# Four edits in a graph network kernel: later row loads, tests on tiles of their own, one test moved between passes, and degree columns one slot later

## The chip, the cores and the metric

The kernel runs on one core of a Trainium2 chip. The metric is the device time of one execution in microseconds (us), and the median of several is compared. A core has a matrix engine (PE), a vector engine (DVE), a scalar engine (ACT), a general engine (GpSimd, POOL in the profile) and SyncE (SP), which here only issues DMA transfers. Each engine works through its own queue in order and waits on semaphores for the others.

## The reference, cut to what matters

There are 16 graphs with 1024 nodes of 128 features, and a dense adjacency of zeros and ones. Two blocks follow each other, each with a residual and a layer norm:

```python
# block 0: four gated layers per graph
for i in range(4):
    hw = einsum('bnc,cd->bnd', h, weight[i])
    m = einsum('bjn,bjd->bnd', adj, hw)
    h = gru_cell(m, h, w_ih[i], w_hh[i], b_ih[i], b_hh[i])
# block 1: neighbours are thinned row by row, then three mean-aggregation layers
for n in range(N):                       # earlier rows change later rows
    row = carry[n]; num = sum(row)
    sf = (num + 1) // 2 if num > 10 else 1
    rm = row & (cumsum(row) % sf == 0) & (num > 1)
    carry[n] = row & ~rm; carry[:, n] &= ~rm
deg = clip(sum(adj_d, -1), 1)
out = (adj_d @ x / deg) @ Wr + x @ Wx + b
h1 = batchnorm(relu(out / norm(out)))    # h2 and h3 likewise from h1 and h2
y = concat(h1, h2, h3) @ Wl + bl
```

The thinning of block 1 needs only the adjacency, not the result of block 0.

## The kernel before, in words

The program takes fast paths that hold only if every adjacency entry is 0 or 1. So it tests the adjacency in tiles of 128 rows by 1024 columns: one DVE instruction per tile (a `scalar_tensor_tensor`, `look`, line 1982) writes a flag into a column of `bad`, and a general routine runs at the end if any flag is set. Eight tiles a graph are tested, spread over three stages. Their only product is that flag.

**Gated stage** (`Gated` and `FixPoint`, to about 1345 us). `Gated.run` goes over pairs of graphs (`b0`), four layers, and two streams `s`, one graph each. `layer` multiplies the state by the adjacency tiles `h_a` (L1093: the state is split into a rounded part h_hi and a rest h_lo, the h_lo products follow the h_hi products) and then runs the gates (L1105 on PE, L1115 to L1124 on ACT, L1118, L1120 and L1133 on DVE, h_zh and h_h L1128 to L1134 on POOL). Between these pieces it calls `aside(n)`. `aside` advances the second program, `FixPoint.steps`, by one yield and runs jobs of the other stream: loads of the next graph's `h_a` and `h_x` (L1011, L1022) on POOL's queue, h_lo of a new graph on POOL (`begin_rows`, L1058), the addition for a finished graph (L1071). `FixPoint` thins the neighbours in 32 blocks of 128 rows of four graphs. Of each block, `load` (L687) brings four row tiles `f_a` (cast to bf16) on POOL's queue into a pool of eight; `keep` and `count` (L731, L739) count along rows; `settle`, `rows` (L868, L870) and `last_u` finish the block one turn later. `rows` gives `f_nr`, which SP stores to DRAM (L871) and reads back transposed for later blocks (`read_back`, L715). One block takes two layers, one of each stream, and 20 yields. In `before`, `last_u` issues the four loads of the block after next as soon as the rows of the old block have been used. The test of the gated stage (`check`, L1013) reads an `h_a` tile that is there for the matmuls, one per two layers: 32 tests, two a graph.

**First pass** (`Sage.first`, `slot`, to about 1855 us). One graph takes 16 slots, and everything is emitted slot by slot in a hand-written order that all five engines keep. In each slot `unit` turns a part of the thinned matrix into `p_at` (L1489 on PE, L1494 on DVE, L1497 on ACT) for the *next* graph and `pack` makes bytes of it on POOL (L1504). For the graph of *now*, `agg` multiplies (slots 0, 1, 3, 4 and 9 to 14), `degree_columns` (slots 3 and 6) turns the row of degrees into columns with four small matmuls (L1559) and takes the reciprocal on DVE (L1561, L1562), `out_first` (slots 5 and 7) makes `p_oa` and `p_ob`, and `scale_rows` (L1394, L1395, slots 6 and 8), `squares` (L1402 on ACT) and `rows` (L1408 to L1413 on DVE) normalise. `turn_x` (slots 6 and 8) transposes the next graph's input (L1424) and ACT copies it out (L1541). `degree_columns`, `turn_x` and `turn_r` share one PSUM buffer, s_tr. Four adjacency tiles a graph are loaded on SP (`load_a`, L1465) into four buffers and tested (L1985).

**Second pass** (`Sage.second`, `slot_second`, to about 2140 us). Eight slots a graph: `out_next` (L1765 to L1771), `chain` (scale and squares), `rows`, `turn_r`, the products with `q_at` (L1808), and `unpack` (L1755 on ACT, L1757 on POOL and DVE), which turns bytes back into `q_at`. Two adjacency tiles a graph go through one buffer `q_a` (loads L1794, tests in slots 3 and 7).

A **third pass** and an output stage follow without tests.

Of the kernel before, what the change touches and what calls it, by code (L numbers as in the profile page):

```python
# [22 lines left out]
B = 16  # L23
# [607 lines left out]
class FixPoint:  # L631
# [110 lines left out]
    def steps(self):  # L742

        nc, G = self.nc, self.G
        for c in range(G):
            self.load(c)
        old = None
        for i, (k, b0) in enumerate(self.todo):
            diag = slice(k * P, k * P + P)

            yield
            if old:
                old.settle()
                old.wide_u(0)
            yield
            if old:
                old.wide_u(1)
                old.rows(0)
            yield
            if old:  # L760
                old.wide_u(2)
                old.rows(1)
            yield
            if old:
                old.rows(2)
                old.wide_u(3)
                old.rows(3)
            a = [self.loaded.pop((i, g)) for g in range(G)]
            pt = self.ps.tile([P, G, P], F32, name="f_pd")
            turned = pt.rearrange("p g n -> p (g n)").bitcast(BF)[:, :G * P].rearrange("p (g n) -> p g n", g=G)  # L770
            for g in range(G):
                nc.tensor.transpose(turned[:, g, :], a[g][:, diag], self.cst["ident_b"])
            yield
            if old:
                old.last_u()

            both = self.small.tile([P, G, P], BF, name="f_both")
            for g in range(G):
                nc.vector.tensor_mul(both[:, g, :], a[g][:, diag], turned[:, g, :])
            nc.gpsimd.affine_select(both, both, pattern=[[0, G], [1, P]], compare_op=ALU.is_gt, fill=0.0,  # L780
                                    base=0, channel_multiplier=-1)
            self.turn(i, 0)
            yield
            rank = self.two.tile([P, G, N], F16, name="f_rank")
            self.keep(i, a[0])
            self.count(i, 0, a[0], rank, pt)
            yield
            yield
            self.turn(i, 1)
            self.keep(i, a[1])  # L790
            yield
            self.count(i, 1, a[1], rank, pt)
            if i == 0:

                for c in range(G, self.LOTS):
                    self.load(c)
            yield
            yield
            yield
            self.turn(i, 2)  # L800
            self.keep(i, a[2])
            self.count(i, 2, a[2], rank, pt)
            yield
            for g in range(G):
                self.read_back(i + 1, g)
            yield
            self.turn(i, 3)
            self.keep(i, a[3])
            self.count(i, 3, a[3], rank, pt)

            num = self.sm[:, 0, 0, :]
            nc.vector.tensor_scalar(num, rank[:, :, N - 1], 1.0, None, op0=ALU.mult)
            q = self.params(num, 0)
            u = self.diag_u(rank[:, :, diag], q)
            if old:
                old.check()
            yield
            x = self.removed(u, q, both)
            yield
            yield  # L820
            pd, num = self.less(x, rank, 1)
            rd = self.small.tile([P, G, P], F16, name="f_rd")
            q = self.params(num, 1, lambda: nc.vector.tensor_sub(rd, rank[:, :, diag], pd))
            u = self.diag_u(rd, q)
            yield
            x = self.removed(u, q, both)
            yield
            old = self.Block(self, i, a, rank, both, x)
            yield
        yield  # L830
        old.settle()
        for n in range(4):
            old.wide_u(n)
            if n < 3:
                yield
            old.rows(n)
        yield
        old.last_u()
        yield
        old.check()  # L840

    class Block:
# [30 lines left out]

        def last_u(self):
            fix = self.fix
            for g in range(fix.G):
                fix.load(fix.G * self.i + g + fix.LOTS)
            self.u = fix.small.tile([P, fix.G, P], F16, name="f_u3", bufs=1)
            fix.diag_u(self.rank[:, :, self.diag], self.q, self.u)

# [43 lines left out]
class Gated:  # L924
# [45 lines left out]
    def prepare(self):  # L970
# [21 lines left out]
            nc.vector.tensor_copy(dst, pt[:, :L0 * 3])  # L992
        nc.vector.tensor_add(self.bs, self.bi, self.bh)

    def stream(self, s):
        return self.Stream(self, s)

    class Stream:
# [9 lines left out]
        def load_adj(self, b, j):  # L1008
            if b < B:
                self.adj[j] = self.top.adjp.tile([P, N], FR, name=f"h_a{self.s}")  # L1010
                self.nc.gpsimd.dma_start(self.adj[j], self.top.adj[b, j * P:(j + 1) * P, :].bitcast(FR))  # L1011

        def check(self, b, j):  # L1013
            junk = self.top.wk.tile([P, N], BF, name="h_junk", bufs=1)
            self.nc.vector.scalar_tensor_tensor(junk, self.adj[j].bitcast(F32), 0.0, self.adj[j].bitcast(F32),
                                                op0=ALU.is_gt, op1=ALU.not_equal,
                                                accum_out=self.top.bad[:, tile_of(b, j):tile_of(b, j) + 1])

        def load_x(self, b):
            if b < B:  # L1020
# [145 lines left out]
    def beside(self, st, ot, l, s, b0, steps):  # L1166


        before = l if s == 0 else l + 1
        if before in (0, L0):  # L1170
            old = not (s == 0 and b0 == 0)
            new = not (s == 1 and b0 + 2 >= B)
            jobs = {5: [], 7: [], 9: []}
            nxt = ot.b + 2 if old else ot.b

            def begin():
                ot.b = nxt
                ot.begin(0)

            if old:  # L1180
                jobs[5].append(lambda: ot.finish(0))
                jobs[7].append(lambda: ot.finish(1))
                jobs[0] = [lambda: ot.load_x(nxt)]
                for j in range(4, NB):
                    jobs.setdefault(j // 2 - 2, []).append(lambda j=j: ot.load_adj(nxt, j))
            if new:
                jobs.setdefault(5 if old else 0, []).append(lambda: ot.begin_rows(nxt))
                jobs[9].append(begin)
        else:
            jobs = {5: [lambda: ot.next_layer(0)], "rest": [lambda: ot.rest(0)],  # L1190
                    7: [lambda: ot.next_layer(1)], 8: [lambda: ot.rest(1)]}

        if l == L0 - 1:

            for j in range(4):
                jobs.setdefault(4, []).append(lambda j=j: st.load_adj(st.b + 2, j))

        checked = []

        def aside(n):  # L1200

            first = n == 7 and before not in (0, L0)
            if not first and n not in ("rest", 8):
                next(steps, None)
            for job in jobs.get(n, ()):
                job()
            if n == 1 and s == 1 and not checked:
                own = l in (0, L0 - 1)
                (st if own else ot).check((st if own else ot).b, l // 2)
                checked.append(l)  # L1210
            if first or n == 8:
                next(steps, None)
        return aside


class Sage:
# [388 lines left out]
    def slot(self, b, t):  # L1605
# [2 lines left out]
        now, nxt = b >= 0, n < B  # L1608

        if nxt:  # L1610
            if t in (0, 2, 8):
                self.load_a(n, (0, 2, 8).index(t) + 3)
            if t in (4, 6):
                self.load_nr(n + 1, (t - 4) // 2)
            if t == 7:
# [15 lines left out]
        if now:  # L1631
# [3 lines left out]
            if t in (0, 1, 3, 4):  # L1635
                f, lo = t // 3, t in (1, 4)
                if not lo:
                    g["pa", f] = bank()
                self.agg(g["pa", f], (self.xh, self.xl)[lo], g["at"], f, range(NB), not lo, lo)
            if t in (5, 7):  # L1640
                self.out_first(b, t // 7)
            if t in (6, 8):
                f = t // 8
                g["o", f] = self.scale_rows(b, f, g.pop(("oa", f)), g.pop(("ob", f)))
            if t in (3, 6):
                self.degree_columns(b, t // 6)
            if t in (7, 9):
                f = t // 9
                g["r", f] = self.rows(b, f, g.pop(("o", f)), g.pop(("ss", f)))
# [14 lines left out]
        if nxt:  # L1664
# [5 lines left out]
                self.turn_x(n, t // 8)  # L1670
            if t in (7, 12):
                self.split_x(n, t // 12)
            if t in (4, 10, 12, 14):
                self.check(n, (4, 10, 12, 14).index(t) + 2)

        if now:
            if t == 2:
# [104 lines left out]
    def slot_second(self, b, t):  # L1782
        nc, g, p = self.nc, self.g.get(b), self.g.get(b - 1)
        acc = lambda b, f: self.acc[:, b, 4 * f:4 * f + 4, :]
        if b < B:
# [2 lines left out]
                self.load_bytes(b + 1, 0)  # L1788
            if t == 3:
                self.load_bytes(b, 1)  # L1790
            if t in (0, 4):
                k = 6 + t // 4
                g["a", k] = self.wk.tile([P, N], F32, name="q_a", bufs=1)
                nc.sync.dma_start(g["a", k], self.adj[b, k * P:(k + 1) * P, :])  # L1794
            if t in (0, 3):
# [38 lines left out]
            self.unpack(b - 1, t + 5)  # L1834
        if t == 5 and b < B:
            self.split(1, g["r", 1], g["rh"], g["rl"])
        if t in (3, 7) and b < B:
            k = 6 + t // 7
            a = g.pop(("a", k))
            look(nc, a.bitcast(BF).rearrange("p (n h) -> p n h", h=2)[:, :, 0], self.bad, a, b, k)  # L1840
        if t == 7 and b < B:
# [229 lines left out]
```

## Time and profile before

| | us |
|---|---|
| median of 3 runs | 2366.65 |
| lowest and highest | 2364.03, 2367.73 |
| the profiled execution | 2359.65 |
| its span in the trace | 2357.6 |

| engine | busy us | share of the span |
|---|---|---|
| PE | 2173.6 | 92% |
| DVE | 1952.1 | 83% |
| ACT | 1327.9 | 56% |
| POOL | 1060.6 | 45% |

All durations come from one profiled execution. A line of a timeline gives the start in us from the span's start, the duration in us, the engine, the line of the program, the operation, what is written and read, and how many were merged; in brackets stands the idle time of the engine ahead of it and what ended it. A line of the list of waits gives engine, tile and line, what was waited for, and then the us in total, how many times, and the longest. A line of the windows by stage gives the stretch, its length, the busy us of PE, PE's weight loads, DVE, ACT and POOL with instruction counts, the granted PE clock, the DMA share and GB/s. The page's chain of the work that ended last holds only one instruction for this kernel (u_y on ACT), so that the stages have to be read one by one.

### The profile page before, as it was taken

What the parts mean: (1) busy time and instruction counts of PE and PEld (TensorE: products, weight loads), DVE (VectorE), ACT (ScalarE), POOL (GpSimd) and SP (SyncE); (2) the same over time, 40 slices, a digit from 0 to 9 for tenths busy, and PEclk for the clock granted to TensorE, in tenths of its full rate; (3) what the DMA queues carried; (4) which work ended last, traced back from release to release, by engine and by line L of the source; (5) the groups of instructions that cost most, each with busy time, mean ns of one, the idle gap of its engine ahead of it and who ended that gap; (6) DMA issues with size and microseconds to landing.
All of it is one profiled execution on the core that took longest, in us unless ns stands there. A gap on an engine that the chain in (4) does not pass through costs nothing. (4 is left out here: it accounts for less than half of the span.)

```text
span 2357.6 us, 33315 instructions
## 1 busy us (share of the span) xinstructions
PE 2173.6 (92%) x10665; PEld 1483.7 (63%) x10665; DVE 1952.1 (83%) x4338; ACT 1327.9 (56%) x3238; POOL 1060.6 (45%) x1092
## 2 busy tenths in 40 slices
PE   6999999999999999999999888888898888888987
PEld 4665655656656656556566467777777666666765
DVE  4998998989989989989989977777777587886777
ACT  3556565655556465565656556556655344445756
POOL 4436346354364363363553265555555245451002
PEclk9999999999999999999999989999999899999989
DMA  7337245263363364271552376666665587775414
GB/s 229 78 80 228 56 122 167 54 196 104 85 202 77 93 191 93 72 216 41 160 153 66 134 256 241 227 233 244 241 241 186 183 288 265 287 264 182 127 39 144
DMA packets 209790, 385.70 MB, mean 164 GB/s; under 512 B 59074, under 2 KB 80228, under 8 KB 209604
## 3 DMA queue, kind: packets, MB, share of 16 engines
q1 hardware_dynamic: 163780, 263.90, 33.1%
q0 software_dynamic: 41472, 117.46, 18.7%
q10 hardware_dynamic: 4352, 2.11, 0.4%
q8 instruction: 86, 1.41, 0.2%
q14 instruction: 100, 0.82, 0.1%
HBM read 307.71 MB, written 109.25 MB: 177 GB/s over the span
## 5 line engine op out<-in xcount | busy, mean ns | idle before, releaser
L1105 PE MATMUL h_g<-h_h,h_wh 128*128 128x512 f32 x768 | 399.3, 601 | 3.0 <-DVE h_r L1118 3.0
L1105 PE MATMUL h_g<-h_ms,h_wi 128*128 128x512 f32 x768 | 392.2, 592 | 0.0
L739 DVE TENSOR_TENSOR_SCAN f_rank<-f_a,f_first,f_pd 128x1024 f16<-128x1024 bf16 x128 | 299.2, 2343 | 3.2
L1093 PE MATMUL h_g<-h_a,h_lo 128*128 128x512 f32 x1024 | 275.3, 408 | 25.6 <-POOL h_lo L1058 25.6
L1134 POOL TENSOR_TENSOR h_h<-h_zh,h_r 128x512 f32<-128x512 f32 x126 | 205.0, 1627 | 194.8 <-DVE h_r L1133 175.7
L1093 PE MATMUL h_g<-h_a,h_hi 128*128 128x512 f32 x1024 | 284.1, 419 | 1.5 <-DMA h_a<-in_adj_dram 1.5
L1105 PEld LDWEIGHTS h_g<-h_ms,h_wi 128*128 128x128 f32 x768 | 145.6, 190 | 183.9 <-issue 166.6
L1504 POOL CAST p_b<-p_at 128x512 uint8<-128x512 f32 x256 | 187.2, 741 | 118.3 <-ACT p_at L1497 48.9
L1093 PEld LDWEIGHTS h_g<-h_a,h_lo 128*128 128x128 f32 x1024 | 195.7, 195 | 69.4 <-POOL h_lo L1058 28.6
L1402 ACT ACTIVATE s_junk<-s_o 128x128 bf16<-128x128 f32 x384 | 113.9, 298 | 213.5 <-DVE s_o L1395 202.6
L1093 PEld LDWEIGHTS h_g<-h_a,h_hi 128*128 128x128 f32 x1024 | 190.2, 190 | 62.3 <-issue 20.1
L1128 POOL TENSOR_TENSOR h_zh<-h_z,h_h 128x512 f32<-128x512 f32 x63 | 80.1, 1272 | 320.6 <-ACT h_z L1124 320.6
L1096 ACT COPY h_ms<-h_g 128x512 f32<-128x512 f32 x128 | 73.7, 576 | 224.8 <-PE h_g L1093 179.4
L1105 PEld LDWEIGHTS h_g<-h_h,h_wh 128*128 128x128 f32 x768 | 129.1, 190 | 85.8 <-issue 65.2
L1121 ACT ACTIVATE h_r<-h_r,h_bi 128x512 f32<-128x512 f32 x128 | 92.3, 721 | 131.2 <-DVE h_r L1120 131.0
L916 ACT ACTIVATE f_u<-f_rank,f_q 128x128 f16<-128x128 f16 (+7 forms) x128 | 110.5, 866 | 76.6 <-DVE f_rank L854 76.6
L1494 DVE SCALAR_TENSOR_TENSOR p_at<-p_nr,p_u 128x128 fp32r<-128x128 bf16 (+1 forms) x192 | 103.4, 546 | 46.9 <-PE p_u L1489 46.9
L1497 ACT ACTIVATE p_at<-p_u 128x512 fp32r<-128x512 f32 (+3 forms) x160 | 74.5, 470 | 119.9 <-DVE p_at L1494 77.9
L687 POOL DMA_DIRECT2D f_a<-in_adj_dram x128 | 69.6, 545 | 122.9 <-DVE f_nr L870 57.0
L1768 PE MATMUL q_ob<-s_wxp,q_xt 128*128 128x256 f32 x512 | 122.9, 383 | 0.0
L1489 PE MATMUL p_u<-ident_b,p_nr 128*128 128x128 bf16 x1024 | 103.4, 230 | 18.6 <-ACT p_at L1497 16.1
L893 ACT ACTIVATE f_pd<-f_rank,f_q 128x128 f32<-128x128 f16 x128 | 59.1, 462 | 106.7 <-DVE f_q L701 103.5
(260 smaller groups left out, 5049.3 us busy)
## 6 DMA issues: line engine op xcount, KB each, us to landing
h_a<-in_adj_dram POOLq DMA_DIRECT2D x128, 512.0 KB, 7.9
f_a<-in_adj_dram POOLq DMA_DIRECT2D x128, 256.0 KB, 7.3
e_nr<-f_nr SPq DMA_DIRECT2D x128, 256.0 KB
p_nr<-e_nr SPq DMA_DIRECT2D x32, 1024.0 KB
p_a<-in_adj_dram SPq DMA_DIRECT2D x64, 512.0 KB
s_at<-p_b SPq DMA_DIRECT2D x32, 512.0 KB
s_ag<-s_ag SPq DMA_DIRECT2D x64, 256.0 KB
q_agi<-s_ag SPq DMA_DIRECT2D x32, 512.0 KB
```

The source lines that it names most:

```text
L739: nc.vector.tensor_tensor_scan(out, a, other[:, 0, 0:1].to_broadcast([P, N]), start, op0=ALU.add, op1=ALU.bypass)
L916: nc.scalar.activation(u[:, :n1], rank[:, g, :n1], AF.Abs, bias=q[:, 1, g:g + 1], scale=q[:, 0, g:g + 1])
L1093: nc.tensor.matmul(pm[f], part[:, j, :], st.adj[j][:, half[f]], start=(j == 0 and n == 0), stop=(j == NB - 1 and n == 1))
L1105: nc.tensor.matmul(pg, lhs, rhs, start=(i == 0), stop=(i == len(mm) - 1))
L1121: nc.scalar.activation(r, r, AF.Tanh, bias=bias(self.bi, 2))
L1128: aid.tensor_tensor(zh, z, h, ALU.mult)
L1134: aid.tensor_tensor(h, zh, r, ALU.subtract)
L1402: self.nc.scalar.activation(junk, o[:, i, :], AF.Square, accum_out=ss[:, i:i + 1])
L1489: nc.tensor.matmul(pu[:, i * P:(i + 1) * P], v[:, 4 * f + i, j * P:(j + 1) * P], self.cst["ident_b"], start=True, stop=True)
L1494: nc.vector.scalar_tensor_tensor(at[:, j, c0:c0 + low], v[:, j, c0:c0 + low], 0.0, pu[:, :low], op0=ALU.is_lt, op1=ALU.is_lt)
L1504: self.nc.gpsimd.tensor_copy(g["b", f][:, j, :], g["at"][:, j, f * HF:(f + 1) * HF].bitcast(F32))
L1768: nc.tensor.matmul(pb[:, i], g["xt"][:, f, blk], self.wxp, start=(i % 2 == 0), stop=False)
```

## The change

It makes four edits. (1) In `FixPoint.steps` the four row loads are issued from the step that follows the second count of the block, instead of from `last_u` earlier in the same block: the same tiles, six yields later. (2) In the gated stage the 32 tests read tiles of their own: `load_test` loads a float32 tile on SP's queue into one buffer `h_test`, at `aside(3)` of stream 0's layer, and `check` tests it at `aside(1)` of stream 1's layer, where the old test stood. The `h_a` loads lose their `bitcast` of the source to float32r. (3) Of the second pass's two tests per graph the one in slot 3 goes, with its load, and the first pass gets one more: it now loads at slots 0, 3, 5, 8 and 12 and tests at slots 2, 4, 10, 12 and 14. (4) The second `degree_columns` of a graph moves from slot 6 to slot 7, ahead of `out_first`.

```diff
@@ FixPoint.steps
             yield
             yield
+            if old:
+                for g in range(G):
+                    self.load(G * (i - 1) + g + self.LOTS)
             yield
             self.turn(i, 2)
@@ Block.last_u
             fix = self.fix
-            for g in range(fix.G):
-                fix.load(fix.G * self.i + g + fix.LOTS)
@@ Gated
+    def load_test(self, n):
+        if n < B * 2:
+            self.test = self.wk.tile([P, N], F32, name="h_test", bufs=1)
+            self.nc.sync.dma_start(self.test, self.adj[n // 2, n % 2 * P:(n % 2 + 1) * P, :])
+
+    def check(self, n):
+        junk = self.wk.tile([P, N], BF, name="h_junk", bufs=1)
+        look(self.nc, junk, self.bad, self.test, n // 2, n % 2)
@@ Stream.load_adj
-                self.nc.gpsimd.dma_start(self.adj[j], self.top.adj[b, j * P:(j + 1) * P, :].bitcast(FR))
-
-        def check(self, b, j):
...
+                self.nc.gpsimd.dma_start(self.adj[j], self.top.adj[b, j * P:(j + 1) * P, :])
@@ Gated.beside, aside
+            if n == 3 and s == 0:
+                self.load_test(b0 // 2 * L0 + l)
             if n == 1 and s == 1 and not checked:
-                own = l in (0, L0 - 1)
-                (st if own else ot).check((st if own else ot).b, l // 2)
+                self.check(b0 // 2 * L0 + l)
                 checked.append(l)
@@ Sage.slot
-            if t in (0, 2, 8):
-                self.load_a(n, (0, 2, 8).index(t) + 3)
+            if t in (0, 3, 5, 8):
+                self.load_a(n, (0, 3, 5, 8).index(t) + 3)
...
+            if t == 7:
+                self.degree_columns(b, 1)
             if t in (5, 7):
                 self.out_first(b, t // 7)
...
-            if t in (3, 6):
-                self.degree_columns(b, t // 6)
+            if t == 3:
+                self.degree_columns(b, 0)
...
-            if t in (4, 10, 12, 14):
-                self.check(n, (4, 10, 12, 14).index(t) + 2)
+            if t in (2, 4, 10, 12, 14):
+                self.check(n, (2, 4, 10, 12, 14).index(t) + 2)
@@ Sage.slot_second
-            if t in (0, 4):
-                k = 6 + t // 4
+            if t == 0:
+                k = NB - 1
...
-        if t in (3, 7) and b < B:
-            k = 6 + t // 7
+        if t == 7 and b < B:
+            k = NB - 1
```

More of the change, by code (lines that the diff above doesn't have):

```diff
@@ L1010, in load_adj @@
                 self.adj[j] = self.top.adjp.tile([P, N], FR, name=f"h_a{self.s}")
-                self.nc.gpsimd.dma_start(self.adj[j], self.top.adj[b, j * P:(j + 1) * P, :].bitcast(FR))
-        def check(self, b, j):
[L1014 to L1017, printed above, removed]
+                self.nc.gpsimd.dma_start(self.adj[j], self.top.adj[b, j * P:(j + 1) * P, :])
         def load_x(self, b):
```

## The prediction

> **What bounds the kernel now.** First the windows by stage: share of time in which each engine is busy.
>
> ```profile
> 400.00:600.00 200.00, 195.93 (x773) 119.92 (x772) 181.11 (x378) 116.86 (x219) 92.83 (x92) 0.98 0.42 111
> 1500.00:1600.00 100.00, 90.08 (x628) 72.28 (x626) 71.34 (x184) 58.71 (x164) 55.28 (x65) 0.95 0.70 250
> 1900.00:2000.00 100.00, 87.14 (x465) 67.94 (x464) 80.20 (x130) 45.75 (x147) 49.12 (x35) 1.00 0.81 278
> ```
>
> PE is the busiest engine in the gated stage (98%), the first pass (90%) and the second (87%), so the end moves by what happens to PE's gaps. The list of waits, second, says what ends them:
>
> ```profile
> PE h_g L1093 <- POOL h_lo L1058: 25.6, 7, 3.7
> PE s_tr L1424 <- DVE s_rdeg L1561: 29.9, 15, 2.0
> PE q_ag L1808 <- DVE q_at L1757: 22.3, 14, 1.9
> ```
>
> Each has one place per graph or pair of graphs. The timelines there, third. Gated stage, POOL at one change of graphs:
>
> ```profile
> 351.41 0.53 POOL L687 DMA_DIRECT2D f_a<-in_adj_dram  x1 [2.16 <-DMA h_a<-in_adj_dram]
> ...
> 356.71 0.53 POOL L687 DMA_DIRECT2D f_a<-in_adj_dram  x1 [1.01 <-DMA h_a<-in_adj_dram]
> 357.24 0.65 POOL L780 TENSOR_SCALAR_AFFINE_SELECT f_both<-f_both 128x512 bf16<-128x512 bf16 x1
> 357.84 1.26 POOL L1071 TENSOR_TENSOR h_x<-h_x,h_w 128x512 f32<-128x512 f32 x1
> 359.07 2.49 POOL L1058 TENSOR_TENSOR h_lo<-h_x,h_hi 128x512 fp32r<-128x512 f32 x2
> ```
>
> Four row loads wait in turn for older loads to land; h_lo stands behind them, and PE (ready at 356.7) behind h_lo until 360.38. First pass, PE and ACT in slots 6 and 7 of one graph:
>
> ```profile
> 1598.99 0.25 PE L1559 MATMUL s_tr<-s_one,p_rl 1*128 1x1 f16 x4
> 1601.23 0.66 PE L1424 MATMUL s_tr<-ident,p_s 128*128 128x128 f32 x4 [1.99 <-DVE s_rdeg L1561]
> ...
> 1601.95 1.11 PE L1581 MATMUL p_oa<-s_wr,s_ag 128*128 128x128 f32 x8
> ```
> ```profile
> 1601.14 0.31 ACT L1402 ACTIVATE s_junk<-s_o 128x128 bf16<-128x128 f32 x1 [3.38 <-DVE s_o L1395]
> ...
> 1602.57 0.57 ACT L1541 COPY p_xt<-s_tr 128x512 f32<-128x512 f32 x1
> ```
>
> PE idles 1.99 us for the one s_tr buffer; ACT's copy of that buffer comes only after the squares (L1402). Second pass, DVE:
>
> ```profile
> 2008.88 1.39 DVE L1985 SCALAR_TENSOR_TENSOR q_a<-q_a 128x1024 bf16<-128x1024 f32 x1
> ...
> 2010.58 1.23 DVE L1410 TENSOR_TENSOR s_ss<-s_ss,mask 128x4 f32<-128x4 f32 x1
> 2011.91 1.40 DVE L1413 SCALAR_TENSOR_TENSOR s_r<-s_o,s_ss 128x512 f32<-128x512 f32 x1
> ...
> 2015.00 2.16 DVE L1985 SCALAR_TENSOR_TENSOR q_a<-q_a 128x1024 bf16<-128x1024 f32 x1 [0.24 <-DMA q_a<-in_adj_dram]
> ```
>
> Here PE idles 1.57 + 0.48 = 2.05 of the 17.16 us of a graph. What sets 17.16 is a loop through DVE and ACT: scale, squares, rows, unpack, test, scale.
>
> [...] POOL idles 2.16 us ahead of an f_a issue. [...] L1410, 0.17 us elsewhere, takes 1.23 while POOL runs q_rl.
>
> **Row loads.** Still 128, at 0.55 us each on POOL; none is saved. In an ordinary block they move from 428.1, where each waits for DVE to free its buffer (57.0 us of POOL idle, off the path), to behind the next layer's second h_h on POOL, 444.2: 16 us later, past two h_zh and two h_h, with 2.2 us of issuing ahead of POOL's next idle time of over 10 us. At a change of graphs POOL then goes from the eight h_a issues (end 349.3) to f_both 0.65, h_x 1.26, h_lo 2.49: h_lo ready by 353.6, before PE asks at 356.7. That removes 7 x 3.66 = 25.6 us. DVE could take the gap's place, but after it DVE stands idle anyway (1.46 us at 370.88, 2.36 at 375.82), so I count no loss. At a pair's first layer the four loads now come between h_a issues: 2.1 us plus four landings of 1.3 (spacing of h_a landings in the trace) put the last h_a at about 376, needed about 378. Rows land some 10 us before their transposes (L772). Cost 0; if that slack is gone, 1 to 2 us at each of 8 places.
>
> **Own test tiles.** 32 tests of 1.75 us (L1015) stay in their DVE slots. New are 32 SP loads of 512 KB. SP issues each right after the f_rt loads or f_nr stores of the block before (f_rt at 446.3, test at 462.7), some 16 us ahead of its test, so DVE's new wait, with f_w and f_nr queued behind it, costs 0. But at a change of graphs SP reaches the load at 347.4, in the middle of the h_a loads, whose fourth already ends a PE wait at 356.22 (0.2 to 0.56 us in four of seven changes). One more load in the same engines delays it by up to 1.3: I take 1.0 x 7 = 7 us given back, bounds 0 and 9. The very first such load competes with the prologue: 1 us (0 to 1.3). Gated stage: -25.6 + 7 + 1 = -17.6.
>
> **Degree columns.** The four L1559 matmuls go behind turn_x. turn_x then starts at 1598.99 and no longer waits, but L1559 in slot 7 needs s_tr back from ACT's copy of turn_x's result. The copy ends at 1602.57 + 0.57 = 1603.14, since the squares ahead of it wait for DVE's s_o as before. PE, done with the unit of slot 7 by about 1599.8, has nothing else in its queue and stands 3.4 us: out_first starts at 1603.14 + 0.05 + 0.18 = 1603.37 instead of 1601.95, 1.42 later, and all that follows hangs on it. Further, DVE's degree ops now stand ahead of rows(0), which slip from 1602.75 to 1603.9, into POOL's p_xl (1603.73, 1.53 long)[...]; then s_r would come 0.2 us after ACT wants it. I take 1.62 x 15 graphs = +24.3 us. Bounds: -2.0 a graph (if the wait simply vanishes) and +2.8 (every operation of rows(0) blocked, and squares behind it).
>
> **Tests of the passes.** First pass: one test more in slot 2, 1.22 + 0.08 us on DVE, in slots 2 to 6 where DVE idles 0.56 + 0.31 + 1.53 = 2.4 us (before L1551, L1494 and L1494). It hides; bound 0.65 us a graph if POOL stretches it. Its p_a is issued ten slots ahead; the k = 3 tile, now tested in slot 4, some 9 us ahead. Four buffers still suffice, SP gains one issue a graph. Only in the very first graph, where PE waits for ACT and DVE, do I charge 1.5 us. Second pass: one q_a load and one test fewer. The test of 1.39 was beside ACT's squares: rows(1) starts only 0.17 us earlier. But that lets L1410 go before POOL's q_rl (2010.51) and L1413 run when q_rl ends (2011.78), so s_r is there at 2012.47 instead of 2013.31: 0.84. The remaining test loses its DMA wait, 0.24 to 0.55. Together 1.2 x 15 graphs = -18 us. Bounds: 0.55 a graph without the help of the lock (-8), and PE's own 2.05 (-31).
>
> **Sum.** -17.6 + 24.3 + 1.5 - 18 = -9.8 us. Against the profiled execution of 2359.65 (span 2357.6 and 2.05 around it) 2349.9. The median of the runs shown, 2366.65, is 7.0 higher; the same difference gives 2357.
>
> **Rivals.**
> A, degree columns cost no wait (chance 0.07): 30 us gained instead of 24.3 lost, 2366.65 - 64 = 2303. For it: 1.99 us stands in the trace at that place. Against it: the copy on ACT is later than the reciprocal on DVE.
> B, the second pass yields only its direct part, 8 us (0.22): 2367, no change. For it: the test lay beside ACT; against: L1410's 1.23.
> C, slower (0.21): DVE's rows(0) in slot 7 locked behind POOL's p_xl and the packs, 2.8 us a graph, +42 instead of +24.3: 2375. It decides from 2.3 us a graph, where the first pass eats the other two gains. For it: L1408 took 0.56 instead of 0.16 beside a pack at 1607.28. Against it: ACT has its own work until 1606.65.
> The forecast, near 2357, has 0.50.
>
> **Range.** C's end and half of the spread to A give 2338 to 2376, which leaves out A and the tails, under 2 in 10. Because gains of 36 us meet losses of 26, signs are mixed; the likeliest case alone spans 2348 to 2362. Measurement tells 0.2% (4.7 us) from no change. Faster: the forecast and A, 0.57; same: B, 0.22; slower: C, 0.21.
>
> **What would show it.** PE L1093 waiting for POOL h_lo is gone, its wait for DMA h_a is 1 to 2 us at changes of graphs. PE's 1.99 us before L1424 turns into about 3.4 us before the degree matmul, ended by ACT p_xt. The first pass takes about 31.3 us a graph instead of 29.6 (from one L1561 of a graph, 1594.05, to the next, 1623.68), the second about 16.0 instead of 17.16. A first pass that is shorter than before would prove the degree step wrong; PE waits for DVE h_r of over 1 us in the gated stage would prove the first.

## The result, and the profile after

The changed kernel takes 2382.85 us (median of 5 runs, 2381.98 to 2387.69), the kernel before 2366.65. The ratio is 1.0073, 95% interval 1.0057 to 1.0089: slower by 0.7%, where 2357 was forecast. The profiled execution of the changed kernel took 2382.46 us, with a span of 2380.7.

Five marks on PE split the two traces by stage: the end of the last L1093 product (L1097 after the change), the first and last p_u, the first q_oa and the last q_ag.

| stage | before us | after us | difference | forecast |
|---|---|---|---|---|
| gated, to its last product | 1330.6 | 1331.8 | +1.2 | -17.6 |
| first pass, first to last p_u | 481.5 | 525.5 | +44.0 | +25.8 |
| second pass, first q_oa to last q_ag | 283.0 | 263.3 | -19.7 | -18.0 |
| all between and behind | 262.5 | 260.1 | -2.4 | 0 |

The two spans differ by 23.1 us, the medians by 16.2, because the profiled execution of before was 7.0 us below its median.

Of the list of waits, three lines of the changed kernel (engine, tile and line, what was waited for, us in total, times, longest) answer to those of before:

```profile
PE s_tr L1564 <- ACT p_xt L1546: 51.9, 15, 3.5
PE h_g L1097 <- DMA h_a<-in_adj_dram: 27.9, 18, 4.7
PE q_ag L1815 <- POOL q_at L1764: 5.6, 15, 1.9
```

No h_lo stands in the list any more, as foretold. But h_a has taken its place: PE waits 27.9 us for it (1.5 before), against the 25.6 us for h_lo that are gone, and the wait at s_tr, now ended by ACT's copy p_xt, has grown from 29.9 to 51.9. Only the second pass has lost a wait for good.

The same change of graphs as before, POOL's timeline:

```profile
358.03 0.60 POOL L1077 DMA_DIRECT2D e_sum<-h_x  x1 [0.30 <-POOL h_x L1075]
...
367.35 0.96 POOL L1026 DMA_DIRECT2D h_x<-in_x_dram  x1 [4.69 <-DMA e_sum<-h_x]
368.31 1.09 POOL L1021 DMA_DIRECT2D h_a<-in_adj_dram  x2
369.36 2.15 POOL L687 DMA_DIRECT2D f_a<-in_adj_dram  x4
371.44 0.59 POOL L1021 DMA_DIRECT2D h_a<-in_adj_dram  x1
372.47 0.53 POOL L1021 DMA_DIRECT2D h_a<-in_adj_dram  x1 [0.43 <-DMA h_x<-in_x_dram]
```

and PE's, one layer after the place where it used to wait:

```profile
375.91 1.62 PE L1097 MATMUL h_g<-h_a,h_hi 128*128 128x512 f32 x6
381.04 0.79 PE L1097 MATMUL h_g<-h_a,h_hi 128*128 128x512 f32 x1 [3.51 <-DMA h_a<-in_adj_dram]
```

The e_sum store is issued at 358.03 behind eight h_a loads and lands at 366.78. POOL waits for it with the h_x load, and everything behind that is late. Then the four f_a loads go ahead of the last two h_a loads. Their landings, each about 1.25 us after the one before, come at 373.46 and 374.72 (h_a), 375.95 to 379.66 (f_a), and 381.00 and 382.25 (h_a), while PE is through with six of the eight tiles at 377.5.

First pass, one graph, timeline of PE and ACT around the second degree columns:

```profile
1620.89 1.11 PE L1586 MATMUL p_oa<-s_wr,s_ag 128*128 128x128 f32 x8
...
1627.14 0.57 ACT L1546 COPY p_xt<-s_tr 128x512 f32<-128x512 f32 x1
...
1627.76 0.24 PE L1564 MATMUL s_tr<-s_one,p_rl 1*128 1x1 f16 x4 [3.46 <-ACT p_xt L1546]
1627.93 2.08 PE L1586 MATMUL p_oa<-s_wr,s_ag 128*128 128x128 f32 x8
```

The wait of 3.46 us and its cause are the forecast ones. What was not forecast stands in the last line: the same eight matmuls that took 1.11 us in slot 5 take 2.08 in slot 7, after the wait. p_ob and p_u slow down likewise. The window in the middle of the pass says it as a whole (us, PE, PE's loads, DVE, ACT, POOL, granted clock, DMA share, GB/s):

```profile
1500.00:1600.00 100.00, 86.86 (x583) 70.17 (x581) 70.80 (x181) 55.15 (x155) 53.17 (x60) 0.91 0.67 240
```

The granted clock is 0.91 where it was 0.95, and 628 matmuls of the window have become 583.

Second pass, DVE's timeline at rows(1):

```profile
2013.30 0.17 DVE L1415 TENSOR_TENSOR s_ss<-s_ss,mask 128x4 f32<-128x4 f32 x1
2013.57 1.70 DVE L1418 SCALAR_TENSOR_TENSOR s_r<-s_o,s_ss 128x512 f32<-128x512 f32 x1
```

As foretold, the small product takes 0.17 us instead of 1.23, since it is through before POOL's q_rl (2013.44, 1.27 us); now L1418 is held up by it (0.69 us at 2008.61, away from q_rl). From the start of the one to the end of the other it is 1.97 us instead of 2.73.

### The profile page after: what moved, and what is told of

The parts are those of the page before. It is cut to its first block, busy times and chain, and to the rows that moved or that the text cites. A ratio compares the mean times of both kernels' runs of the same rounds, so it can differ in the third digit from the quotient of the medians.

```text
span 2380.7 us, 33249 instructions
## 1 busy us (share of the span) xinstructions
PE 2193.1 (92%) x10665; PEld 1496.1 (63%) x10665; DVE 1935.1 (81%) x4338; ACT 1329.3 (56%) x3238; POOL 1060.4 (45%) x1092
## 5 line engine op out<-in xcount | busy, mean ns | idle before, releaser
L1097 PE MATMUL h_g<-h_a,h_hi 128*128 128x512 f32 x1024 | 288.5, 421 | 27.9 <-DMA h_a<-in_adj_dram 27.9
L1138 POOL TENSOR_TENSOR h_h<-h_zh,h_r 128x512 f32<-128x512 f32 x126 | 199.2, 1581 | 195.5 <-DVE h_r L1137 172.5
L1097 PE MATMUL h_g<-h_a,h_lo 128*128 128x512 f32 x1024 | 272.9, 405 | 0.0
L1097 PEld LDWEIGHTS h_g<-h_a,h_hi 128*128 128x128 f32 x1024 | 189.8, 190 | 93.5 <-DMA h_a<-in_adj_dram 36.2
L1509 POOL CAST p_b<-p_at 128x512 uint8<-128x512 f32 x256 | 197.5, 781 | 107.9 <-ACT p_at L1502 48.0
L1097 PEld LDWEIGHTS h_g<-h_a,h_lo 128*128 128x128 f32 x1024 | 195.9, 194 | 40.6
L1499 DVE SCALAR_TENSOR_TENSOR p_at<-p_nr,p_u 128x128 fp32r<-128x128 bf16 (+1 forms) x192 | 103.0, 544 | 26.7 <-PE p_u L1494 25.4
L1494 PE MATMUL p_u<-ident_b,p_nr 128*128 128x128 bf16 x1024 | 104.6, 231 | 20.3 <-ACT p_at L1502 15.9
L1424 POOL TENSOR_TENSOR q_rl<-s_r,q_rh 128x512 fp32r<-128x512 f32 x32 | 58.0, 1812 | 132.8 <-ACT q_rh L1423 96.2
```

Of the source, the lines that this page charges most:

```text
L1097: nc.tensor.matmul(pm[f], part[:, j, :], st.adj[j][:, half[f]], start=(j == 0 and n == 0), stop=(j == NB - 1 and n == 1))
L1138: aid.tensor_tensor(h, zh, r, ALU.subtract)
L1494: nc.tensor.matmul(pu[:, i * P:(i + 1) * P], v[:, 4 * f + i, j * P:(j + 1) * P], self.cst["ident_b"], start=True, stop=True)
L1499: nc.vector.scalar_tensor_tensor(at[:, j, c0:c0 + low], v[:, j, c0:c0 + low], 0.0, pu[:, :low], op0=ALU.is_lt, op1=ALU.is_lt)
L1509: self.nc.gpsimd.tensor_copy(g["b", f][:, j, :], g["at"][:, j, f * HF:(f + 1) * HF].bitcast(F32))
```

## The experiments

First, each part of the change stands alone on the kernel before.

**Degree columns alone**, the hunks of `degree_columns`:

```diff
+            if t == 7:
+                self.degree_columns(b, 1)
             if t in (5, 7):
                 self.out_first(b, t // 7)
...
-            if t in (3, 6):
-                self.degree_columns(b, t // 6)
+            if t == 3:
+                self.degree_columns(b, 0)
```

> The kernel before with the degree columns moved to slot 7, nothing else. Theory (wait and clock): PE idles some 3.4 us before the degree matmul of each of 15 graphs and runs the next 2 to 3 us of matmuls at half clock (p_oa x8 takes 2.1 instead of 1.1 us), so the first pass (first to last p_u, 481.6 us before) takes about 40 us more, 2405. Rival (wait only, as predicted): p_oa takes 1.1 us, the pass takes 22 to 26 us more, 2390. Rival (the extra test in slot 2 is part of the 43.9 us): 44 minus some 10 to 20, 2392 to 2400, with slow matmuls present.

Measured: 2396.47 us against 2367.50, ratio 1.0126 (1.0109 to 1.0143), +29 us; first pass 518.3 us.

```profile
PE s_tr L1559 <- ACT p_xt L1541: 52.3, 15, 3.9
```

The wait is there without any other part of the change, and so are the slow matmuls (after 14 of the 15 waits). The time lies between the first two theories and in the range of the third, which puts part of the 44 us down to the extra test. The stage itself has spread: with untouched instructions it took 481.5 us in the profile of before, 487.1 and 488.7 in those of the next two experiments, in which the matmuls after the old 2-us wait were slow in 12 graphs of 15 instead of 9.

**Row loads alone**:

```diff
+            if old:
+                for g in range(G):
+                    self.load(G * (i - 1) + g + self.LOTS)
             yield
             self.turn(i, 2)
@@ last_u
-            for g in range(fix.G):
-                fix.load(fix.G * self.i + g + fix.LOTS)
```

> The kernel before with the row loads issued six yields later, nothing else. Theory (the late row loads push the last two h_a loads back): the 7 waits on h_lo go (25.6 us), and PE waits about as long for DMA h_a one layer later, so the end of the gated stage stays within 5 us of 1330.6, 2362 to 2371. Rival (the test loads on SP's queue cause the h_a waits): h_a waits of PE below 5 us in total, the gated stage 20 to 26 us shorter, 2342 to 2346.

Measured: 2354.91 us, ratio 0.9950 (0.9935 to 0.9966), 12.6 us faster; the gated stage ends at 1316.6, 14.0 earlier. PE waits 19.3 us for h_a. Neither theory: the row loads alone give back about half of what they win, not all. POOL's timeline at the same change of graphs shows the difference to the changed kernel:

```profile
361.32 0.97 POOL L1023 DMA_DIRECT2D h_x<-in_x_dram  x1 [2.49 <-DMA e_sum<-h_x]
```

The e_sum store lands 6.56 us after its issue, not 8.75, and POOL waits 2.49 us, not 4.69. PE still comes too early for the last two tiles:

```profile
372.50 1.62 PE L1094 MATMUL h_g<-h_a,h_hi 128*128 128x512 f32 x6
...
376.38 0.50 PE L1094 MATMUL h_g<-h_a,h_hi 128*128 128x512 f32 x1 [0.76 <-DMA h_a<-in_adj_dram]
```

**Own test tiles alone** (the hunks of `load_test`, `check`, `load_adj` and `aside`):

```diff
...
+            if n == 3 and s == 0:
+                self.load_test(b0 // 2 * L0 + l)
             if n == 1 and s == 1 and not checked:
-                own = l in (0, L0 - 1)
-                (st if own else ot).check((st if own else ot).b, l // 2)
+                self.check(b0 // 2 * L0 + l)
```

> The kernel before with the 32 tests of the gated part on tiles of their own, nothing else. Theory of the row loads: the gated stage changes by -1 to +4 us, PE's waits for DMA h_a grow by less than 6 us, 2366 to 2371. Rival (the test loads compete with the h_a loads, 1.0 us at each of 7 changes, as predicted, or more): 7 to 25 us longer, 2374 to 2392.

Measured: 2366.01 us, ratio 0.9996 (0.9987 to 1.0006). By themselves the 32 loads, with the `h_a` loads without their bitcast, cost nothing: the stage ends at 1330.5 as before, and PE waits 1.3 us in all for h_a (1.5 before).

**One test moved between the passes**:

```diff
-            if t in (0, 2, 8):
-                self.load_a(n, (0, 2, 8).index(t) + 3)
+            if t in (0, 3, 5, 8):
+                self.load_a(n, (0, 3, 5, 8).index(t) + 3)
@@
-            if t in (4, 10, 12, 14):
+            if t in (2, 4, 10, 12, 14):
@@ slot_second
...
-            if t in (3, 7) and b < B:
+            if t == 7 and b < B:
```

> The kernel before with one test a graph moved from the second pass to the first, nothing else. Theory: the second pass (first q_oa to last q_ag, 281.2 us) is some 19 us shorter, period 15.9 us, and the first pass stays within 5 us of 481.6, so 2347 to 2352. Rival (the extra test in slot 2 costs the first pass 10 to 20 us): 2357 to 2367, with first-pass periods near 31.5 us.

Measured: 2352.80 us, ratio 0.9941 (0.9925 to 0.9958). Second pass 263.6 us, period 15.90, as expected. The first pass takes 491.6, 10.1 us more, with 10 slow graphs where the profile of before has 9; its prologue (first p_u to first product with p_xh) takes 20.1 instead of 18.0. So the extra test costs more than nothing there: by the medians about 19.4 - 14.7 = 5 us. The other half of the 10.1 is within the spread of untouched passes (481.5 to 488.7).

The four parts sum to +29.0 - 12.6 - 1.5 - 14.7 = +0.2 us. The change costs 16.2. So two parts harm each other, and the stages say where: 1316.6 with the row loads alone, 1331.8 with all parts, both before the passes begin. Two runs on the changed kernel ask which of the two pieces does it.

**Row loads behind the last h_a loads**, in the changed kernel:

```diff
-            if old:
-                for g in range(G):
-                    self.load(G * (i - 1) + g + self.LOTS)
             yield
             self.turn(i, 2)
...
             for g in range(G):
                 self.read_back(i + 1, g)
             yield
+            if old:
+                for g in range(G):
+                    self.load(G * (i - 1) + g + self.LOTS)
```

> The changed kernel with the four row loads two yields later, so that at a pair's first layer they follow the last two h_a loads on POOL's queue instead of standing ahead of them; elsewhere nothing changes its order. Theory (the four row loads, 2.15 us of issuing and four landings of 1.25 us, hold the last two h_a back): those land some 5 us earlier, PE's waits for DMA h_a fall from 27.9 to below 8 us, the gated stage ends near 1304 instead of 1331.8, 2350 to 2360. Rival (the wait for the e_sum store and the test loads are the cause, the row loads' place is not): waits of 18 to 28 us remain, the gated stage ends at 1322 to 1332, 2373 to 2384.

Measured: 2344.42 us, ratio 0.9910 (0.9894 to 0.9926) to the kernel before. The gated stage ends at 1291.5, 40.3 us earlier. Of POOL's timeline and of PE's waits:

```profile
360.19 0.96 POOL L1026 DMA_DIRECT2D h_x<-in_x_dram  x1 [4.91 <-DMA e_sum<-h_x]
361.15 2.15 POOL L1021 DMA_DIRECT2D h_a<-in_adj_dram  x4
363.25 1.64 POOL L687 DMA_DIRECT2D f_a<-in_adj_dram  x3
```
```profile
PE h_g L1097 <- DMA h_a<-in_adj_dram: 2.5, 4, 0.8
```

The wait for e_sum is still there, the wait for h_a is not. The order of eight issues on one queue is worth 40 us, more than the 25.4 us of waits that it removes. The rest is PE's clock. Windows of the gated stage from 100 us to its last product, in the kernel before and here:

```profile
100.00:1330.60 1230.60, 1200.28 (x4750) 731.62 (x4749) 1125.06 (x2261) 710.19 (x1325) 582.77 (x582) 0.99 0.44 120
100.00:1291.50 1191.50, 1185.55 (x4751) 721.10 (x4750) 1124.21 (x2262) 710.19 (x1326) 582.10 (x582) 1.00 0.48 137
```

The stage is 39.1 us shorter than before. PE's idle time falls by 24.4 us, from 30.3 to 5.9, and its busy time by the other 14.7, though the matmuls are the same: the granted clock is now full throughout.

**No test load at the seven changes of graphs**, in the changed kernel:

```diff
-            if n == 3 and s == 0:
+            if n == 3 and s == 0 and (l or not b0):
                 self.load_test(b0 // 2 * L0 + l)
```

> The changed kernel without the test load at the seven changes of graphs: the test there reads the tile of the layer before once more, so seven of the 32 tiles of the gated part are not tested. Theory (the test load, in the middle of the eight h_a loads, delays the e_sum store, and with it everything on POOL up to the last h_a): POOL's wait for e_sum falls from 4.7 to about 2.5 us, PE's waits for DMA h_a from 27.9 to 17 to 20 us, the gated stage from 1331.8 to 1315 to 1320, 2366 to 2372. Rival (what differs from the row loads alone is the h_a loads without their bitcast, or the tests' waits on DVE): the gated stage stays at 1327 or more, 2377 to 2385.

Measured: 2366.53 us, ratio 1.0007 (0.9999 to 1.0015). The gated stage ends at 1317.6, and

```profile
363.52 0.96 POOL L1026 DMA_DIRECT2D h_x<-in_x_dram  x1 [2.55 <-DMA e_sum<-h_x]
```

PE waits 18.1 us for h_a: all as the first theory has it, and the numbers of the row loads alone. So seven loads of 512 KB cost 14 us together with the row loads, and nothing without them, where PE waits for h_a only 1.3 us in all.

The rest is about the first pass.

**PE kept busy in its wait**, in the changed kernel: nine bf16 matmuls into the free p_oa buffer, overwritten by the real ones.

```diff
-        pa = self.ps1.tile([P, 4, C], F32, name="p_oa")
+        pa = self.pa7 if f else self.ps1.tile([P, 4, C], F32, name="p_oa")
...
             if t == 7:
+                self.pa7 = self.ps1.tile([P, 4, C], F32, name="p_oa")
+                for i in range(9 * nxt):
+                    nc.tensor.matmul(self.pa7.rearrange("p a b -> p (a b)"), self.cst["ident_b"],
+                                     self.g[n]["nr"][:, 7, :HF], start=True, stop=True)
                 self.degree_columns(b, 1)
```

> The changed kernel with nine bf16 matmuls of 512 columns put into PE's wait ahead of the second degree columns, their result overwritten by p_oa. Theory (the idle time lowers the clock of what follows): the degree matmul starts as late as before (idle plus fillers 3.4 to 3.9 us), but p_oa x8 takes 1.1 to 1.4 us instead of 2.08 and the other matmuls of slot 7 shrink likewise, 2 to 2.7 us a graph, first pass 485 to 500 us, 2343 to 2358. Rival (the slow matmuls have another cause, or DVE and ACT set the period anyway): first pass within 8 us of 525, 2375 to 2390.

Measured: 2356.51 us, ratio 0.9959 (0.9944 to 0.9973); first pass 495.4 us, 30.1 less than the changed kernel. PE's timeline of one graph:

```profile
1614.60 2.12 PE L1648 MATMUL p_oa<-p_nr,ident_b 128*128 128x512 bf16 x8 [0.72 <-DVE s_o L1399]
...
1617.34 0.23 PE L1564 MATMUL s_tr<-s_one,p_rl 1*128 1x1 f16 x4 [0.62 <-ACT p_xt L1546]
1617.51 1.16 PE L1586 MATMUL p_oa<-s_wr,s_ag 128*128 128x128 f32 x8
```

The degree matmul starts as late as it did, yet p_oa takes 1.16 us: work without any use makes the kernel 26 us faster. So the idle time, not the matmuls themselves, had lowered PE's clock.

**ACT's copy ahead of the squares**, in the changed kernel:

```diff
+            if t == 6 and nxt:
+                self.turn_x(n, 0)
             if t in (6, 8):
                 g["ss", t // 8] = self.squares(g["o", t // 8])
...
-            if t in (6, 8):
+            if t == 8 or t == 6 and not now:
                 self.turn_x(n, t // 8)
```

> The changed kernel with one order altered: in slot 6 the transposition of the next graph's input and ACT's copy of it come ahead of ACT's squares. Theory (the degree columns stand behind that copy): PE's waits on ACT p_xt, 15 x 3.46 = 52 us, go, out_first waits some 0.7 us for the p_oa buffer instead, p_oa x8 takes 1.1 us again, and the first pass falls from 525.5 to 440 to 460 us, 2305 to 2320. Rival (the first pass is bound by the loop through DVE and ACT, the wait on the copy only being where PE stands in it): another wait of about 3 us takes its place, the pass stays above 500, 2360 or more.

Measured: 2347.66 us, ratio 0.9924 (0.9906 to 0.9941); first pass 489.5 us, 36.0 less. The wait for p_xt shrinks to 6.8 us in all, but its place is partly taken. PE's timeline:

```profile
1643.63 0.23 PE L1564 MATMUL s_tr<-s_one,p_rl 1*128 1x1 f16 x4 [0.45 <-ACT p_xt L1546]
...
1649.21 2.97 PE L1571 MATMUL p_ag<-p_at,p_rh 128*128 128x512 f32 x8 [1.85 <-ACT p_rh L1423]
1655.75 2.09 PE L1571 MATMUL p_ag<-p_at,p_rh 128*128 128x512 f32 x8
```

Neither theory fits in full: the copy was the cause of the wait, but 1.85 us of it return 5.6 us later, where PE waits for p_rh, the end of the chain from s_o over squares and rows. After 14 of 15 such waits PE is slow again: these eight products take 2.97 us here, the next eight, after no wait, 2.09.

**All that helped, together**, on the kernel before: row loads behind h_a, the test moved, degree columns in slot 7 with the copy ahead, the gated tests on h_a as they were.

```diff
             for g in range(G):
                 self.read_back(i + 1, g)
             yield
+            if old:
+                for g in range(G):
+                    self.load(G * (i - 1) + g + self.LOTS)
...
+            if t in (2, 4, 10, 12, 14):
+                self.check(n, (2, 4, 10, 12, 14).index(t) + 2)
...
+            if t == 7:
+                self.degree_columns(b, 1)
...
+            if t == 6 and nxt:
+                self.turn_x(n, 0)
```

> The kernel before with the row loads behind the last h_a loads, one test a graph moved to the first pass, the degree columns in slot 7 with ACT's copy ahead of the squares, and the gated tests on h_a as before. If the theories of the wait on the copy and of the order of the row loads hold and the parts add up: gated stage to about 1302, first pass 440 to 460, second pass 261 us, 2270 to 2300. If the rivals hold: 2330 or more.

Measured: 2304.93 us, ratio 0.9747 (0.9730 to 0.9764). The second pass, 263.1, is about as expected; the gated stage, 1290.6, is 11 us shorter than expected, for it gains the clock as well as the waits; the first pass, 488.8, is 29 us or more longer, for the reason just told.

**The same with the degree columns in slot 6, as before** (and without the reordered copy):

```diff
-            if t == 7:
-                self.degree_columns(b, 1)
...
-            if t == 3:
-                self.degree_columns(b, 0)
+            if t in (3, 6):
+                self.degree_columns(b, t // 6)
```

> The kernel before with the row loads behind the last h_a loads and one test a graph moved to the first pass; the degree columns stay in slot 6. Theory (in the first pass the loop through DVE and ACT takes over once PE's wait is gone, so the old place of the degree columns loses little): first pass 484 to 492 us against 488.8 with the degree columns moved and the copy ahead, 2300 to 2310. Rival (the old wait of 1.99 us and the slow matmuls after it cost their full 3 us a graph): 510 us or more, 2325 or more.

Measured: 2308.87 us, ratio 0.9761 (0.9744 to 0.9778). PE's old wait, 15 times 2.0 us, is back; the first pass takes 496.2, 4 us more than expected. So with its own obstacle out of the way the move of the degree columns wins about 4 us by the medians, and that is not clear of the noise: the two intervals overlap.

Two edits of the combined kernel ask what bounds its first pass. **Scaling ahead of the unit's p_at on DVE**:

```diff
+        if now and t in (6, 8):
+            f = t // 8
+            g["o", f] = self.scale_rows(b, f, g.pop(("oa", f)), g.pop(("ob", f)))
         if nxt:
             self.unit(n, t)
...
-            if t in (6, 8):
-                f = t // 8
-                g["o", f] = self.scale_rows(b, f, g.pop(("oa", f)), g.pop(("ob", f)))
```

> The combined kernel with DVE's scaling (s_o, slots 6 and 8) ahead of the unit's p_at instead of behind it. Theory (that chain bounds the pass): s_o starts 0.7 to 0.9 us earlier, PE's wait on p_rh falls from 1.9 to about 1 us, the pass is 8 to 14 us shorter, 2290 to 2297. Rival (p_at, now later, is what ACT, POOL and PE want first): no gain, or up to 10 us longer, 2302 to 2315.

Measured: 2271.74 us, ratio 0.9605 (0.9589 to 0.9621), the fastest of all, 94 us below the kernel before. First pass 454.0, that is 34.8 us less than combined, where 8 to 14 were expected. One line of PE's timeline from the combined kernel, then one from this:

```profile
1602.35 3.59 PE L1567 MATMUL p_ag<-p_at,p_rh 128*128 128x512 f32 x8 [1.85 <-ACT p_rh L1419]
```
```profile
1581.45 2.12 PE L1567 MATMUL p_ag<-p_at,p_rh 128*128 128x512 f32 x8 [0.82 <-ACT p_rh L1419]
```

The wait falls by 1.03 us, as the theory says. The larger part of the gain is that a wait of 0.82 us leaves PE's clock alone: 3.59 - 2.12 = 1.47 us. In sum 2.50 a graph, near the difference of the two periods, 28.36 and 30.72 us.

**Short tests**, 8 columns of each tile of the first pass:

```diff
-        look(self.nc, self.wk.tile([P, N], BF, name="p_junk", bufs=1), self.bad, self.g[b].pop(("a", k)), b, k)
+        look(self.nc, self.wk.tile([P, N], BF, name="p_junk", bufs=1)[:, :8], self.bad,
+             self.g[b].pop(("a", k))[:, :8], b, k)
```

> The combined kernel with each test of the first pass cut to 8 of 1024 columns, so that it leaves out nearly all of those five tests a graph (6.5 us of DVE). Theory (what bounds the first pass with the copy ahead is the chain from p_ob over s_o, squares and rows to p_rh, which has no test in it): the pass falls by less than 8 us from 488.8, 2297 to 2306. Rival (DVE's load bounds the pass): 15 us or more shorter, below 2290.

Measured: 2289.35 us, ratio 0.9682 (0.9663 to 0.9700); first pass 472.0 us, 16.8 less: more than the one theory says, and the time is that of the other.

```profile
PE p_ag L1568 <- ACT p_rh L1419: 29.5, 16, 1.9
```

But the wait is what it was in the combined kernel, to the tenth. Most graphs take either 30.49 us, near the 30.72 of the combined kernel, or 28.90; in the latter the matmuls after the same wait run at full speed. So 6.5 us less of DVE's work save, by the former, about 0.2 us a graph directly, and the rest is again the clock, which here stayed up after 6 of the 15 waits. The place of the wait in time has a part in it: 30.49 is 0.23 less than the 30.72 of the combined kernel, and from graph to graph the slow products get shorter by about as much (3.63, 3.40, 3.21, 3.03, 2.82 and 2.63 us in six graphs in a row), while in the combined kernel they stay between 3.58 and 3.68. The last section takes this up. Why the clock stayed up in just these six graphs is not settled.

## Why the prediction was wrong

**Row loads.** That h_lo no longer stops PE was right (7 waits of 3.66 gone). The step that failed is "the last h_a at about 376, needed about 378", with "Cost 0" behind it. It counted the issues and landings of the four row loads, but left out that POOL's h_x load, at the head of that group, waits for the e_sum store, which itself lands behind eight h_a loads (4.69 us of POOL idle in the profile after). The last h_a landed at 382.25. With the row loads alone, both times are off by some 2 us. That run is 1.74 us ahead of the kernel before at the layer in front (352.19 for 353.93). Its last h_a landed at 376.33, which is 378.1 in the time of before. PE was through with six tiles at 374.12, or 375.9, and asked for the eighth some 0.2 us later: it began this layer 5.6 us earlier than in the kernel before (372.50 + 1.74 for 379.85), not 3.66, because with the wait the slow products behind it went too. That the row loads' place is what makes PE wait is shown by the run with them behind h_a: 27.9 us of waits become 2.5, though POOL still waits 4.91 for e_sum.

**Own test tiles.** "One more load in the same engines delays it by up to 1.3: I take 1.0 x 7 = 7 us given back". Alone they cost nothing (ratio 0.9996). With the row loads they cost 14 us, 2 for each change: the load holds back the e_sum store by some 2.2 us, and every load behind it. The place of the harm was wrong, and the price comes from two parts together and is not the sum of what each costs alone. Together gated +1.2 instead of -17.6: 18.8 us of the miss.

**The value of the h_lo waits** was mis-sized too, in the other direction: removing them cleanly brings 1330.6 - 1291.5 = 39.1 us, not 25.6. The h_lo products took 628 ns each (median) soon after the wait and 392 otherwise, so that a wait of 3.66 costs about 39.1 / 7 = 5.6. The forecast put this slowing at nothing.

**Degree columns.** The mechanism was right: 3.46 us for 3.4, ended by ACT's p_xt, for the reason given. The term was mis-sized: 1.62 a graph, +24.3, of which 0.2 a graph, for rows(0) beside POOL's p_xl, was the author's estimate. Measured +29.0 by the medians of the part alone; by the profiles 525.5 - 491.6 = 33.9 on top of the moved test, 2.3 a graph. What was missing is the clock: the wait grew by 1.47, and matmuls now ran slowly after all 15 waits instead of 9 (in four graphs p_oa only in part, 1.36 to 1.82 us). Windows of the first pass before, with the degree columns alone, and in the changed kernel:

```profile
1349.30:1831.10 481.80, 426.29 (x2958) 341.44 (x2958) 350.15 (x921) 282.10 (x786) 273.57 (x317) 0.94 0.67 236
1349.30:1867.80 518.50, 442.06 (x2958) 356.85 (x2958) 356.96 (x921) 281.80 (x786) 266.33 (x317) 0.90 0.62 219
1350.40:1876.20 525.80, 446.63 (x2958) 360.31 (x2958) 371.35 (x953) 282.31 (x787) 280.79 (x317) 0.89 0.65 232
```

The part alone adds 20.9 us of idle time to PE, where the forecast's 1.42 x 15 make 21.3. Beside it the same 2958 matmuls take 15.8 us longer at the lower clock, for which the forecast had nothing. In the changed kernel it is 23.7 and 20.3. With PE kept busy 30 of the 44 us of the first pass are gone. Rival C, with the slower end, had another cause: L1415 took 0.89 us beside POOL's p_xl (0.17 at 1636.36, away from it), but s_r was there at 1630.7, nearly 3 us before ACT turned to it at 1633.50. That the total came to lie on C's side does not make it right.

**Moved test.** Second pass -19.7 for -18, period 15.90 for 16.0, by the mechanism given. The first pass was charged 1.5 us for the extra test; the part alone shows 10.1 in the profiles, some 5 by the medians. This and the degree columns make the first pass's 18.2 us: 8.6 and 9.6 by single profiles, a split that the spread of the stage blurs.

**The sum.** -9.8 us was forecast; 18.8 + 18.2 - 1.7 - 2.4 = 32.9 us of misses by the profiles lead to +23.1, of which 7 is the profile of before lying under its median.

## What to carry to other kernels

When a load is moved on a queue, follow the queue from the first instruction that can wait, and compare the time of the last landing with the time of need; here what was issued ahead of the needed load mattered more than how much was issued (the order of eight issues was worth 40 us, 32 more loads alone cost nothing). Cost a wait of PE as its length and the slow matmuls behind it (the h_lo wait of 3.66 us cost about 5.6), and try to make it short enough to leave the clock alone (0.82 us did, 1.85 did not in 14 of 15 graphs) before trying to remove it. Run parts alone as well as together: here two parts that cost -12.6 and -1.5 us alone gave about nothing together.

## What the runs showed of the hardware

PE's clock fell after most waits of about 2 us, and stayed up after those below 1 us. In the first pass of these kernels, matmuls after a wait of 0.6 to 0.8 us ran at full speed in each of 15 graphs (p_rh wait of 0.82, scaling first), and so with fillers; after 1.9 to 2.0 us slowly in 9 of 15 (before), 14 (copy first), 15 (combined) and 9 (short tests); after 3.5 us in 15 of 15 (changed kernel). Slowly is 2.08 us for 1.11 (p_oa x8), and the trace records a granted clock of 0.50 there instead of 1.00. In the traces of the kernel before and of the changed kernel (50 and 58 records of the clock) it changes only at moments that lie whole multiples of 3.413 us apart, to within 5 ns. Here are two graphs of the kernel before, with waits of 2.00 and 1.99 us, in steps between such moments:

```profile
1473.79:1477.20 3.41, 1.41 (x18) 1.21 (x17) 2.23 (x5) 0.29 (x2) 0.61 (x1) 1.00 1.04 405
1477.20:1480.62 3.42, 3.42 (x20) 3.00 (x19) 2.01 (x5) 2.19 (x11) 1.12 (x1) 0.50 0.17 68
...
1596.67:1600.08 3.41, 2.57 (x27) 2.14 (x26) 1.88 (x4) 1.07 (x2) 1.01 (x3) 1.00 1.05 404
1600.08:1603.50 3.42, 2.27 (x21) 2.03 (x22) 2.42 (x9) 2.33 (x11) 0.38 (x1) 1.00 0.65 258
1603.50:1606.91 3.41, 2.88 (x24) 2.52 (x24) 1.92 (x3) 2.33 (x11) 3.02 (x3) 1.00 0.07 30
```

The first wait falls into one step, PE idles 2.00 of its 3.41 us, and the clock of the next step is 0.50. The second is split, 0.84 and 1.15 us of idle time, and the clock stays at 1.00. Counted over the first passes of the kernel before and of the changed kernel, 241 steps ran at full clock. PE idled less than 1.3 us in 214 of them, and half clock followed on one; it idled longer in 27, and half clock followed on 26. No run moved a wait on purpose to test this, so these are counts from two traces, not something proved by an experiment. They fit the periods above: the combined kernel's 30.72 us are nine times 3.413, by which each wait would meet the same place in such a step, while the 30.49 us of the short tests slide by 0.23 a graph; that is an estimate.

The slow clock also goes with the spread of a stage of unchanged instructions, which took 481.5 to 488.7 us from one kernel to the next with 9 to 12 slow graphs. That sets a limit to what one profile can tell of a stage.
